# One attention block's first MLP matrix, batch 0: seven products of blocks in place of eight

## The chip, the cores and the metric

The kernel runs on one core of a Trainium2 chip. The time is the device time of one execution in microseconds (us), median of several runs. The engines are TensorE (PE in the profile; its weight loads are PEld), VectorE (DVE), ScalarE (ACT), GpSimd (POOL) and SyncE (SP), which here only issues DMAs. Each engine executes its own instructions in the order in which they are written; semaphores order them against the other engines.

## What is computed

One block of cross-attention with an MLP, in float32, for a batch of 4, 512 rows, width 512, 16 heads of 32:

```
x   = layer_norm(hidden, ln1_w, ln1_b)
q   = x @ q_w + q_b;   k = enc @ k_w + k_b;   v = enc @ v_w + v_b
p   = softmax(q k^T / sqrt(32)) per head, masked;   out = (p v) @ cproj_w + cproj_b
hid = out + hidden
y   = layer_norm(hid, ln2_w, ln2_b)
y   = gelu(y @ fc_w + fc_b)            # fc: 512 -> 2048
out = hid + y @ proj_w + proj_b        # proj: 2048 -> 512
```

## The kernel before

**Units.** Attention is cut into 16 weeks `w` (a batch `b` and four of its heads), each with 4 units (128 query rows, `qt`); unit number u = 4w + qt. In a unit, `scores` makes four 128x512 score products on TensorE into one PSUM tile `sc` (line 259), VectorE takes mask and minimum from it (263), ScalarE exponentiates (267), and `turn` transposes in blocks of 32 on VectorE (282, 290, 291); in odd units ScalarE also spreads the reciprocal sums (`rr`, 289). Two units' results are exchanged across partitions by sixteen DMAs of SyncE (`copies`, 325) into the tile `pT`, of which there is one, and `attend` (342) multiplies them with `v` two units or more later; VectorE then normalises (`oT`, 347), which frees `pT` for the next exchange. In the weeks from 5 to 12 there is an attend ahead of every even unit.

**Filler.** Between the units TensorE does the rest: `prep_k`, `prep_q`, `prep_v` of later weeks (215, 225, 237), the output projection `cproj` (383), the turning of normalised rows (156), and the MLP of batch 0 and half of fc and proj of batch 1: `fc` (449) and `proj` (459). Lists `first[w]` and `later[w]` name these items with a planned cost (`CHAIN` = 3.4, `TURN` = 0.5). Where the list is a tuple, its parts go to the four units as written; otherwise `run` (725) hands out items while half of the next cost fits into what is due. `some(n)` takes the next n items of the MLP's own list.

**fc before.** A chain `fc(b, f)` makes 128 of the 2048 columns: four 128x512 products in one PSUM tile of the ring `acc` (four banks), then one gelu on ScalarE straight from PSUM into `gT` (450). Weights come through a ring of eight slots `mlp_w`; `load_mlp` (441) is called after each chain and loads into the slots that are through. Exp and gelu need different tables on ScalarE; each change shows as an ACT_TABLE_LOAD.

**Norm of batch 0.** In unit 20, statistics on VectorE (125), then GpSimd takes the reciprocal root (`rs`, 133), VectorE normalises (147), and in unit 21 TensorE turns the four parts (`ln2_turn`); ScalarE and VectorE write `yT` from them (161, 159). On GpSimd's queue stand also `v_bias` (249), `add_row` (354), stores of `h` (386, 465) and loads of the mask (191).

**Last stage.** After attention, `last_mlps` does the rest of batches 1 to 3 by blocks: a product of 2x2 blocks with seven block products in place of eight (Strassen's scheme in Winograd's form). `fc_pair` (541) takes two chains at once: sums of weight blocks (`sum_wa`, lines 481 and 484, on VectorE), sums of blocks of `yT` (`y_sums`, 641), seven products of 128x256 (553), a copy of the first to `p1` (564), four adds on VectorE (531), four gelus of 128x256 (557). `project` (584) does the second matrix alike (593).

The lines that say how seven products make four blocks, in the code before (`product(o, a, y)` is two matmuls):

```python
product(q1[:, 0], a11, y11)
product(q62[:, 1], a12, y21)
product(q62[:, 0], s2, t2)
add(nc.vector, uc, q62, p1[:, None, :].broadcast_to([P, 2, HL]))
product(q75[:, 0], s3, t3)
product(q75[:, 1], s1, t1)
add(nc.vector, u34, q75, uc[:, :1].broadcast_to([P, 2, HL]))
add(nc.vector, uc[:, 0], q75[:, 1], u34[:, 0])
product(q43[:, 1], s4, y22)
product(q43[:, 0], a22, t4)
add(nc.vector, h, q43, u34)
```

Of the kernel before, what the change touches and what calls it, by code (L numbers as in the profile page):

```python
# [52 lines left out]
def xattn_block(ctx: ExitStack, tc: tile.TileContext, x, encT, mask, q_w, k_w, v_w, c_w, fc_w, p_w, vecs, rows, out):  # L53
# [3 lines left out]
    def pools(stack, **bufs):  # L57
        return [stack.enter_context(tc.tile_pool(name=n, bufs=k)) for n, k in bufs.items()]
# [28 lines left out]
    pb = pbt.rearrange("p (c i n) -> p c i n", c=NF // 2, i=2)  # L87
    pt = ptt.rearrange("p (s c n) -> p s c n", s=3, c=NF // 2)

    def k_q(w, i):  # L90
        n = w % 4 * 2 + i
        return pbt[:, n * D : (n + 1) * D]
# [18 lines left out]
        return ptt[:, n * D : (n + 1) * D].rearrange("p (d f) -> p d f", d=ND)  # L111

    S = {}
    count = [0, 0, 0]
    Q = [nc.sync]

    def acc_tile(name):
        return ps_acc.tile([P, D], F32, tag="acc", name=name)
# [315 lines left out]
    def load_mlp():  # L434

        while count[0] < len(weights) and (count[0] < MW or weights[count[0] - MW][3] < count[1]):
            name, b, f, _ = weights[count[0]]
            w = mlp_w(count[0])
            if name == "fc":
                w = w.rearrange("p (d f) -> p d f", d=ND)  # L440
            Q[0].dma_start(out=w, in_=fc_w[:, f, :, :] if name == "fc" else p_w[ts(f, P), :])
            S[name + "w", b, f] = w
            count[0] += 1

    def fc(b, f):
        q, k = divmod(f, FQ)
        acc = acc_tile(f"accf_{b}_{f}")
        for d in range(ND):
            nc.tensor.matmul(acc, S["fcw", b, f][:, d, :], S["yT", b][:, d, :], start=(d == 0), stop=(d == ND - 1))  # L449
# [20 lines left out]

    NP = NF // 2
    HL = L // 2

    def sub(o, x0, x1):  # L480
        nc.vector.tensor_tensor(o, x0, x1, ALU.subtract)  # L481

    def a_sums(a11, a12, a21, a22, s1, s2, s3, s4):
        nc.vector.tensor_tensor(s1, a21, a22, ALU.add)
        sub(s3, a11, a21)
        sub(s2, s1, a11)
        sub(s4, a12, s2)

    def b_sums(b11, b12, b21, b22, t1, t2, t3, t4):
        sub(t1, b12, b11)  # L490
        sub(t2, b22, t1)
        sub(t3, b22, b12)
        sub(t4, b21, t2)


    wa = [gt[:, i * 2048 : i * 2048 + 1024].rearrange("p (i d f) -> p i d f", i=2, d=ND) for i in range(2)]
# [14 lines left out]
        b_sums(b11, b12, b21, b22, pt[:, 0, c], pt[:, 1, c], b12, pt[:, 2, c])  # L511

    def last_mlps():
        last, ring = pools(ctx, last=1, ring=2)
        ps_last = ctx.enter_context(tc.tile_pool(name="ps_last", bufs=4, space=PSUM))
        ys = last.tile([P, 4, 2, HL], F32, tag="ys", name="ys")
# [7 lines left out]
        def half_tile(name):  # L524
            return ps_last.tile([P, 2, HL], F32, tag="half", name=name)

        def acc_half(name):
            return acc_tile(name).rearrange("p (i l) -> p i l", i=2)

        def add(engine, o, x0, x1):  # L530
            engine.tensor_tensor(o, x0, x1, ALU.add)  # L531

        def y_blocks(b):
            return [S["yT", b][:, 2 * k : 2 * k + 2, j * HL : (j + 1) * HL] for k in range(2) for j in range(2)]
# [6 lines left out]
        def fc_pair(b, c, first, sums):  # L541
            a11, a12, a21, a22 = (wa[c % 2][:, i, 2 * k : 2 * k + 2] for i in range(2) for k in range(2))
            y11, y12, y21, y22 = y_blocks(b)
            s1, s2, s3, s4 = (ws[c % 2][:, i] for i in range(4))
            t1, t2, t3, t4 = (ys[:, i] for i in range(4))
            q1, q62 = (acc_half(f"{n}_{b}_{c}") for n in ("q1", "q62"))
            q75, q43 = (half_tile(f"{n}_{b}_{c}") for n in ("q75", "q43"))
            p1 = ring.tile([P, HL], F32, tag="p1", name=f"p1_{b}_{c}")
            uc, u34, h = (ring.tile([P, 2, HL], F32, tag=n, name=f"{n}_{b}_{c}") for n in ("uc", "u34", "h"))

            def product(o, a, y):
                for k in range(2):
                    nc.tensor.matmul(o, a[:, k], y[:, k], start=(k == 0), stop=(k == 1))  # L553

            def gelu(i, j, src):
                f = 2 * c + i
                nc.scalar.activation(  # L557
                    ga[:, c, i, j * HL : (j + 1) * HL], src, AF.Gelu_apprx_tanh,
                    bias=vec[:, FCB + f : FCB + f + 1], scale=1.0,
                )  # L560

            sums()
            product(q1[:, 0], a11, y11)
            nc.scalar.copy(p1, q1[:, 0])  # L564
            product(q62[:, 1], a12, y21)

            if first:
                product(q43[:, 1], s4, y22)
            product(q62[:, 0], s2, t2)
            add(nc.vector, uc, q62, p1[:, None, :].broadcast_to([P, 2, HL]))  # L570
            gelu(0, 0, uc[:, 1])
            product(q75[:, 0], s3, t3)
            product(q75[:, 1], s1, t1)
            add(nc.vector, u34, q75, uc[:, :1].broadcast_to([P, 2, HL]))
            add(nc.vector, uc[:, 0], q75[:, 1], u34[:, 0])
            gelu(1, 1, uc[:, 0])
            if not first:
                product(q43[:, 1], s4, y22)
            product(q43[:, 0], a22, t4)
            add(nc.vector, h, q43, u34)  # L580
            gelu(1, 0, h[:, 0])
            gelu(0, 1, h[:, 1])
# [58 lines left out]
        def y_sums(b):  # L641
            b_sums(*y_blocks(b), *(ys[:, i] for i in range(4)))

        y_sums(SPLIT)

        half = FIRST * FQ // 2
        for b, pairs, new in (
            (SPLIT, range(half, NP), ()), (SPLIT + 1, range(NP), range(half)), (SPLIT + 2, range(NP), ())
        ):
            for c in pairs:  # L650
                if c in new:
                    for i in range(2):
                        nc.sync.dma_start(out=pb[:, c, i, :], in_=p_w[ts(2 * c + i, P), :])
                fc_pair(b, c, c == pairs[0], lambda: sum_wa(c + 1) if c + 1 < NP else None)
# [132 lines left out]
    mlp += FC(SPLIT, 0) + FC(SPLIT, 1) + PJ(SPLIT, 0) + PJ(SPLIT, 1)  # L787

    def some(n):
        taken, mlp[:n] = mlp[:n], []  # L790
        return taken

    def hid_(b, *ts_):
# [14 lines left out]
    def stat(b, *ts_):  # L808
        return do(lambda: [stat2(b, t) for t in ts_])

    def norm(b, *ts_):
# [133 lines left out]
```

## Time and profile before

| | |
|---|---|
| median of 3 runs | 810.84 us (810.18 to 811.25) |
| the profiled execution's own time | 810.09 us |
| its span, first to last instruction | 808.3 us |
| granted TensorE clock, mean | 0.996 |
| TensorE busy | 791.9 us |
| VectorE, ScalarE, GpSimd busy | 553.6, 360.8, 98.0 us |
| fc of batch 0 on TensorE | from 179.7 us to 387.5 us, between the units |
| last stage | from 558.5 us to the end |

A line of the timeline gives start and length in us, engine, line of the code, operation, the tiles written and read, the shape, how many records were merged, and in brackets how long the engine had stood idle before and what released it. `PE` lines are matmul records; one call of `nc.tensor.matmul` here makes two. SPq lines are DMA issues of SyncE.

### The profile page before, as it was taken

How to read it: one execution, taken by the hardware profiler on the slowest of the kernel's cores; microseconds unless marked ns; L12 is line 12 of the kernel's file. 1: busy time of each engine (PE TensorE's matmuls, PEld its weight loads, DVE VectorE, ACT ScalarE, POOL GpSimd, SP SyncE). 2: the span in 40 equal slices, each digit the busy share in tenths (PEclk: the TensorE clock that was granted, in tenths of full speed). 3: DMA queues.
4: the chain of work that ended last, by engine and by line, in shares of the span. 5: the costliest groups of instructions: out<-in, count | busy, mean ns of one | idle time of the engine just before them, and what ended most of it. 6: DMA issues, size and time to landing. Idle time of an engine off the chain costs nothing.

```text
span 808.3 us, 11790 instructions
## 1 busy us (share of the span) xinstructions
PE 791.9 (98%) x4082; PEld 481.2 (60%) x4082; DVE 553.6 (68%) x1145; ACT 360.8 (45%) x785; POOL 98.0 (12%) x112
## 2 busy tenths in 40 slices
PE   9999999979999999999999999999999999999998
PEld 6545455544454544535554333446888888888887
DVE  3788998876678665877778997636738993368511
ACT  2666755638673646556643469600312330023200
POOL 1110030030000030001131000120050021200011
PEclk9999999989999999999999999999999999999999
DMA  9889989837797877778768799883335330023001
GB/s 329 287 222 244 241 219 265 225 96 185 185 245 176 223 201 191 176 197 201 177 140 218 196 259 226 216 252 117 108 100 181 107 117 14 27 79 92 1 14 39
DMA packets 60955, 137.13 MB, mean 170 GB/s; under 512 B 12464, under 2 KB 15664, under 8 KB 60768
## 3 DMA queue, kind: packets, MB, share of 16 engines
q1 hardware_dynamic: 59472, 132.43, 61.2%
q0 software_dynamic: 896, 2.82, 1.1%
q10 hardware_dynamic: 528, 1.14, 0.7%
q8 instruction: 32, 0.52, 0.3%
q14 instruction: 27, 0.22, 0.1%
HBM read 58.22 MB, written 6.82 MB: 80 GB/s over the span
## 4 chain that ended last, share of the span: by engine, by line
PE 80%; DVE 7%; SPq 7%; DMA 3%; issue 1%; POOL 0%; ACT 0%; DVEq 0%; POOLq 0%
PE q L553 15%; PE accf L449 9%; PE accp L459 8%; PE accc L383 7%; SPq L325 7%; PE av L342 6%; PE sc L259 6%; PE acck L215 4%; PE accq L225 4%; PE accv L237 4%; DVE ptt L263 3%; PE q5p L593 2%; PE q3p L593 2%; PE q7p L593 2%; PE q6p L593 2%; PE q1p L593 2%
## 5 line engine op out<-in xcount | busy, mean ns | idle before, releaser
L267 ACT ACTIVATE ptt<-ptt,mn 128x512 f32<-128x512 f32 x256 | 182.2, 713 | 142.8 <-DVE mn L263 142.6
L263 DVE CUSTOM_DVE_ANT_0 ptt<-sc,mb 128x512 f32<-128x512 f32 x256 | 161.1, 685 | 45.6 <-PE sc L259 45.5
L282 DVE STREAM_TRANSPOSE tb<-ptt 128x1024 f32<-128x1024 f32 x96 | 119.1, 1242 | 10.4 <-ACT ptt L267 8.0
L449 PE MATMUL accf<-yT,pbt 128*128 128x512 f32 x192 | 87.3, 601 | 0.0
L459 PE MATMUL accp<-pbt,gt 128*128 128x512 f32 x192 | 86.5, 600 | 0.0
L259 PE MATMUL sc<-pbt 32*128 32x512 f32 x512 | 73.1, 640 | 4.8 <-DVE mn L263 2.6
L553 PE MATMUL q<-ys,gt 128*128 128x256 f32 x320 | 75.1, 379 | 0.0
L553 PEld LDWEIGHTS q<-ys,gt 128*128 128x128 f32 x320 | 60.8, 190 | 8.3
L449 PEld LDWEIGHTS accf<-yT,pbt 128*128 128x128 f32 x192 | 35.0, 190 | 50.2 <-issue 45.4
L459 PEld LDWEIGHTS accp<-pbt,gt 128*128 128x128 f32 x192 | 35.2, 190 | 48.8 <-issue 45.8
L237 PEld LDWEIGHTS accv<-ptt,xe 128*128 128x128 f32 x512 | 58.9, 192 | 8.2 <-issue 5.4
L237 PE MATMUL accv<-ptt,xe 128*128 128x128 f32 x512 | 60.5, 276 | 0.0
L215 PE MATMUL acck<-xe,ptt 128*128 128x512 f32 x128 | 59.0, 603 | 0.0
L553 PE MATMUL q<-yT,gt 128*128 128x256 f32 x240 | 58.1, 379 | 0.5 <-DVE gt L481 0.5
L225 PE MATMUL accq<-xe,ptt 128*128 128x512 f32 x128 | 58.4, 599 | 0.0
L383 PE MATMUL accc<-wc,oT 128*128 128x512 f32 x128 | 56.6, 596 | 0.0
L249 POOL TENSOR_TENSOR v<-v,row 128x512 f32<-128x512 f32 x16 | 20.4, 1274 | 278.5 <-ACT v L242 278.4
L557 ACT ACTIVATE ga<-uc,vec 128x256 f32<-128x256 f32 x40 | 20.4, 511 | 75.5 <-DVE uc L531 75.5
L553 PEld LDWEIGHTS q<-yT,gt 128*128 128x128 f32 x240 | 45.5, 190 | 7.4 <-DVE gt L481 0.9
L342 PE MATMUL av<-pT,v 128*32 128x256 f32 x768 | 48.1, 392 | 1.6 <-DMA pT<-tb 1.5
L267 ACT ACTIVATION_READ_ACCUMULATOR ptt<-ptt,mn 128x1 f32 x256 | 48.3, 189 | 0.0
L564 ACT COPY p<-q 128x256 f32<-128x256 f32 x20 | 7.1, 354 | 92.0 <-PE q L553 92.0
(121 smaller groups left out, 957.9 us busy)
## 6 DMA issues: line engine op xcount, KB each, us to landing
pT<-tb SPq DMA_DIRECT2D x384, 136.0 KB, 2.4
pbt<-p_w_dram SPq DMA_DIRECT2D x40, 256.0 KB, 3.1
gt<-fc_w_dram SPq DMA_DIRECT2D x40, 256.0 KB, 2.7
gt<-tb SPq DMA_DIRECT2D x64, 136.0 KB, 3.4
xe<-tb SPq DMA_DIRECT2D x56, 136.0 KB, 3.3
pbt<-fc_w_dram SPq DMA_DIRECT2D x24, 256.0 KB, 4.3
ptt<-k_w_dram SPq DMA_DIRECT2D x16, 256.0 KB, 3.9
xe<-encT_dram SPq DMA_DIRECT2D x16, 256.0 KB, 4.8
```

Source lines behind the costliest of these rows:

```text
L215: nc.tensor.matmul(acc, S["wk", w][:, d, :], eT[:, d, :], start=(d == 0), stop=(d == ND - 1))
L225: nc.tensor.matmul(acc, S["wq", w][:, d, :], xT[:, d, :], start=(d == 0), stop=(d == ND - 1))
L237: nc.tensor.matmul(acc[:, ts(t, P)], eT[:, d, ts(t, P)], S["wv", w][:, d, :], start=(d == 0), stop=(d == ND - 1),)
L259: nc.tensor.matmul(sc[:, h, :], qT[r, ts(qt, P)], kT[r, :], start=True, stop=True)
L263: nc.vector.tensor_tensor_reduce(out=s, in0=sc[:, h, :], in1=S["mb", w // NG], scale=1.0, scalar=FMAX, op0=ALU.add, op1=ALU.min, accum_out=mn,
L267: nc.scalar.activation(s, s, AF.Exp, bias=mn, scale=-1.0, accum_out=sums[:, qt, h : h + 1])
L282: nc.vector.transpose(*two_heads[k])
L342: nc.tensor.matmul(av[ts(h, HD), : 2 * P].rearrange(shape, **kw), v[:, t, ts(h, HD)], p[t][h], start=(t == 0), stop=(t == NT - 1),)
L383: nc.tensor.matmul(acc, S["oT", b][:, g, ts(t, P)], wc[:, g, :], start=(g == 0), stop=(g == NG - 1))
L449: nc.tensor.matmul(acc, S["fcw", b, f][:, d, :], S["yT", b][:, d, :], start=(d == 0), stop=(d == ND - 1))
L459: nc.tensor.matmul(acc, gT[q % 2][:, k, ts(t, P)], S["pw", b, q * FQ + k], start=(k == 0), stop=(k == FQ - 1))
L553: nc.tensor.matmul(o, a[:, k], y[:, k], start=(k == 0), stop=(k == 1))
```

## The change

The functions for sums and for seven products move out of `last_mlps` and get one body, `fc_seven`, for both places. fc of batch 0 uses it between the units, in pairs of chains (`fc_by_pair`). The sums of weight blocks are made by GpSimd (`fc_sums`), two pairs ahead; one of the four overwrites a block of the raw weights in their slot. The sums of blocks of `yT` of batch 0 are made half by VectorE and half by GpSimd, at the end of unit 21; one overwrites a block of `yT`. `fc_seven` adds into `g` itself and does the two gelus of 128x512 at its end, in place; in the last stage this replaces the four of 128x256, and the fourth product of a batch's first pair is no longer drawn forward. A pair is planned with 5.95; one list moves an item of fc from week 7 to week 8. The scratch space for GpSimd's own DMAs is set to 4096.

```diff
+    ys = const.tile([P, 3, 2, L // 2], F32, tag="ys", name="ys")
+    wsum = const.tile([P, 2, 3, 2, P], F32, tag="wsum", name="wsum")
...
+    def a_sums(a11, a12, a21, a22, s1, s2, s3, s4, engine=None):
+        add(engine or nc.vector, s1, a21, a22)
+        sub(s3, a11, a21, engine)
+        sub(s2, s1, a11, engine)
+        sub(s4, a12, s2, engine)
...
+    def y_sums(b):
+        y11, y12, y21, y22 = y_blocks(b)
+        e = nc.vector if b else nc.gpsimd
+        sub(ys[:, 0], y12, y11)
+        sub(ys[:, 1], y22, ys[:, 0])
+        sub(y12, y22, y12, e)
+        sub(ys[:, 2], y21, ys[:, 1], e)
...
+    def fc_seven(b, c, g, a, s, half):
+
+        y11, t3, y21, y22 = y_blocks(b)
+        t1, t2, t4 = (ys[:, i] for i in range(3))
+        s1, s2, s3, s4 = s
+        q1, q26 = (acc_half(f"{n}_{b}_{c}") for n in ("q1", "q26"))
+        q57, q34 = (half(f"{n}_{b}_{c}") for n in ("q57", "q34"))
+        p1 = small.tile([P, HL], F32, tag="p1", bufs=1, name=f"p1_{b}_{c}")
+        g = g.rearrange("p i (j l) -> p (i j) l", j=2)
...
+        product(q1[:, 0], a[0][:, 0:2], y11)
+        nc.scalar.copy(p1, q1[:, 0])
+        product(q26[:, 0], a[0][:, 2:4], y21)
+        product(q26[:, 1], s2, t2)
+        add(nc.vector, g[:, 0:4:3], q26, p1[:, None, :].broadcast_to([P, 2, HL]))
+        product(q57[:, 1], s3, t3)
+        product(q57[:, 0], s1, t1)
+        u2 = g[:, 3:4]
+        add(nc.vector, g[:, 1:3], q57, u2.broadcast_to([P, 2, HL]))
+        add(nc.vector, g[:, 3], q57[:, 0], g[:, 2])
+        product(q34[:, 0], s4, y22)
+        product(q34[:, 1], a[1][:, 2:4], t4)
+        add(nc.vector, g[:, 1:3], q34, g[:, 1:3])
+        for i in range(2):
+            f = 2 * c + i
+            h = g[:, 2 * i : 2 * i + 2]
+            nc.scalar.activation(h, h, AF.Gelu_apprx_tanh, bias=vec[:, FCB + f : FCB + f + 1], scale=1.0)
...
+    def fc_sums():
+
+        while count[3] < len(fc_pairs) and count[3] < count[4] + 2:
+            b, c = fc_pairs[count[3]]
+            if ("fcw", b, 2 * c + 1) not in S:
+                return
+            x, y = raw_pair(b, c)
+            s = wsum[:, count[3] % 2]
+            a_sums(x[:, :2], x[:, 2:], y[:, :2], y[:, 2:], s[:, 0], s[:, 1], y[:, :2], s[:, 2], nc.gpsimd)
+            S["ws", b, c] = s[:, 0], s[:, 1], y[:, :2], s[:, 2]
+            count[3] += 1
...
+    def fc_by_pair(b, c):
+        q, k = divmod(2 * c, FQ)
+        fc_seven(b, c, gT[q % 2][:, k : k + 2, :], raw_pair(b, c), S["ws", b, c], acc_half)
+        count[1] += 2
+        count[4] += 1
+        load_mlp()
+        fc_sums()
...
     def FC(b, q):
+        if b < SPLIT:
+            return [(2 * CHAIN * 7 / 8, lambda c=c: fc_by_pair(b, c)) for c in range(q * FQ // 2, (q + 1) * FQ // 2)]
         return [(CHAIN, lambda f=f: fc(b, f)) for f in range(q * FQ, (q + 1) * FQ)]
...
     first[5] = (
-        [k] + stat(0, 0, 1, 2, 3) + rs(0) + x3 + norm(0, 0, 1, 2, 3) + [v], [q] + t2, some(2) + pb_(0), some(2)
+        [k] + stat(0, 0, 1, 2, 3) + rs(0) + do(fc_sums) + x3 + norm(0, 0, 1, 2, 3) + [v], [q] + t2 + do(lambda: y_sums(0)), some(2) + pb_(0), some(2)
     )
...
-    first[7] = [k, q] + x2[:1] + some(2) + x2[1:2] + some(3) + [v]
+    first[7] = [k, q] + x2[:1] + some(2) + x2[1:2] + some(2) + [v]
...
-    first[8] = h_(1, 0, 1) + x2[2:] + [k, q] + x3[:2] + some(1) + x3[2:3] + [v] + x3[3:] + h_(1, 2, 3) + x4
+    first[8] = h_(1, 0, 1) + x2[2:] + [k, q] + x3[:2] + some(2) + x3[2:3] + [v] + x3[3:] + h_(1, 2, 3) + x4
...
-    nc = bacc.Bacc("TRN2", target_bir_lowering=False, num_devices=1)
+    nc = bacc.Bacc("TRN2", target_bir_lowering=False, num_devices=1, dynamic_dma_scratch_size=4096)
```

More of the change, by code (lines that the diff above doesn't have):

```diff
@@ L113, in xattn_block @@
     S = {}
-    count = [0, 0, 0]
+    count = [0, 0, 0, 0, 0]
     Q = [nc.sync]
@@ L443, in load_mlp, with sub, add, b_sums @@
             count[0] += 1
+    NP = NF // 2
+    HL = L // 2
+    def sub(o, x0, x1, engine=None):
+        (engine or nc.vector).tensor_tensor(o, x0, x1, ALU.subtract)
+    def add(engine, o, x0, x1):
+        engine.tensor_tensor(o, x0, x1, ALU.add)
+    def a_sums(a11, a12, a21, a22, s1, s2, s3, s4, engine=None):
[3 more added lines that the diff above has]
+        sub(s4, a12, s2, engine)
+    def b_sums(b11, b12, b21, b22, t1, t2, t3, t4):
+        sub(t1, b12, b11)
+        sub(t2, b22, t1)
+        sub(t3, b22, b12)
+        sub(t4, b21, t2)
@@ new lines, in y_blocks, with acc_half, product @@
+    def y_blocks(b):
+        return [S["yT", b][:, 2 * k : 2 * k + 2, j * HL : (j + 1) * HL] for k in range(2) for j in range(2)]
+    def y_sums(b):
[5 more added lines that the diff above has]
+        sub(ys[:, 2], y21, ys[:, 1], e)
+    def acc_half(name):
+        return acc_tile(name).rearrange("p (i l) -> p i l", i=2)
+    def fc_seven(b, c, g, a, s, half):
[6 more added lines that the diff above has]
+        g = g.rearrange("p i (j l) -> p (i j) l", j=2)
+        def product(o, x, y):
+            for k in range(2):
+                nc.tensor.matmul(o, x[:, k], y[:, k], start=(k == 0), stop=(k == 1))
+        product(q1[:, 0], a[0][:, 0:2], y11)
[15 more added lines that the diff above has]
+            nc.scalar.activation(h, h, AF.Gelu_apprx_tanh, bias=vec[:, FCB + f : FCB + f + 1], scale=1.0)
@@ new lines, in xattn_block, with raw_pair @@
+    fc_pairs = [(b, c) for b in range(SPLIT) for c in range(NP)]
+    def raw_pair(b, c):
+        return [S["fcw", b, 2 * c + i] for i in range(2)]
+    def fc_sums():
[8 more added lines that the diff above has]
+            count[3] += 1
@@ L467, in proj @@
         load_mlp()
[L477 to L493, printed above, removed]
+        fc_sums()
     wa = [gt[:, i * 2048 : i * 2048 + 1024].rearrange("p (i d f) -> p i d f", i=2, d=ND) for i in range(2)]
@@ L513, in last_mlps @@
     def last_mlps():
-        last, ring = pools(ctx, last=1, ring=2)
+        last, = pools(ctx, last=1)
         ps_last = ctx.enter_context(tc.tile_pool(name="ps_last", bufs=4, space=PSUM))
-        ys = last.tile([P, 4, 2, HL], F32, tag="ys", name="ys")
         ga = last.tile([P, NP, 2, L], F32, tag="ga", name="ga")
@@ L525, in half_tile @@
             return ps_last.tile([P, 2, HL], F32, tag="half", name=name)
[L527 to L534, printed above, removed]
         def g_sums(c):
@@ L539, in g_sums, with fc_pair @@
             a_sums(a11, a12, a21, a22, gs[:, 0, c], gs[:, 1, c], a21, gs[:, 2, c])
[L541 to L560, printed above, removed]
-            sums()
[L563 to L582, printed above, removed]
+        def fc_pair(b, c, sums):
+            sums()
+            fc_seven(b, c, ga[:, c], [wa[c % 2][:, i] for i in range(2)],
+                     [ws[c % 2][:, i] for i in range(4)], half_tile)
         def project(b, pairs, sums, turns, middle):
@@ L639, in project @@
                 nc.sync.dma_start(out=out[b, ts(2 + t, P), :HL], in_=hid(1, 0, t))
-        def y_sums(b):
-            b_sums(*y_blocks(b), *(ys[:, i] for i in range(4)))
         y_sums(SPLIT)
@@ L653, in last_mlps @@
                         nc.sync.dma_start(out=pb[:, c, i, :], in_=p_w[ts(2 * c + i, P), :])
-                fc_pair(b, c, c == pairs[0], lambda: sum_wa(c + 1) if c + 1 < NP else None)
+                fc_pair(b, c, lambda: sum_wa(c + 1) if c + 1 < NP else None)
                 if c + 2 < NP:
@@ L789, in some @@
     def some(n):
-        taken, mlp[:n] = mlp[:n], []
+        taken = []
+        while n > 0:
+            n -= 1 if mlp[0][0] == CHAIN else 2
+            taken.append(mlp.pop(0))
+        assert n == 0
         return taken
```

## The prediction

> **What bounds the kernel now.** I read the page's busy shares first, then TensorE's instructions in order of time, then the waits, then the DMA issues of SyncE's queue. TensorE is busy for 791.9 of 808.3 us:
>
> ```profile
> PE 791.9 (98%) x4082; PEld 481.2 (60%) x4082; DVE 553.6 (68%) x1145; ACT 360.8 (45%) x785; POOL 98.0 (12%) x112
> ```
>
> Only 16 us are left in which TensorE does nothing, so a change gains by giving it fewer or shorter products, and loses by making it wait. In the stretch that the change touches, TensorE's timeline (start, length, engine, line, tiles, count, idle before) has nearly no holes:
>
> ```profile
> 204.87 1.14 PE L259 MATMUL sc<-pbt 32*128 32x512 f32 x8
> 205.94 7.13 PE L449 MATMUL accf<-yT,pbt 128*128 128x512 f32 x16
> 213.00 1.93 PE L342 MATMUL av<-pT,v 128*32 128x256 f32 x32
> 214.87 1.14 PE L259 MATMUL sc<-pbt 32*128 32x512 f32 x8
> 215.94 3.70 PE L449 MATMUL accf<-yT,pbt 128*128 128x512 f32 x8
> ...
> 227.84 1.93 PE L342 MATMUL av<-pT,v 128*32 128x256 f32 x32
> ...
> 369.30 1.93 PE L342 MATMUL av<-pT,v 128*32 128x256 f32 x32 [0.98 <-DMA pT<-tb]
> ```
>
> There is a second bound just behind it. Each attend (`av`) frees the one `pT` tile, and SyncE then issues the sixteen DMAs that fill it for the next attend:
>
> ```profile
> 215.45 10.37 SPq L325 DMA_DIRECT2D pT<-tb  x16
> ...
> 355.87 11.39 SPq L325 DMA_DIRECT2D pT<-tb  x16
> ```
>
> A DMA here takes 0.63 us to issue and lands a median 2.4 us later. From the start of one attend to the earliest start of the next: 2.45 (attend 1.86, normalising multiply, until the first issue) + 9.4 (fifteen issues) + 2.4 (landing) + 0.24 (until TensorE starts) = 14.5 us. Where the issue took 11.39 instead of 10.03, the next attend really waited (the 0.98 above). The attends at 213.00 and 227.84 are 14.84 apart: hardly any slack.
>
> **The saving on TensorE.** Two chains of fc (16 records; a call of 128x512 is two of them) take 213.00 - 205.94 = 7.06 us, of which 0.2 belongs to the switch from the score products; 6.86 is pure. A pair by seven products is what the last stage does already:
>
> ```profile
> 570.58 1.89 PE L553 MATMUL q<-yT,gt 128*128 128x256 f32 x8
> 572.31 2.75 PE L553 MATMUL q<-ys,gt 128*128 128x256 f32 x12
> 574.90 1.03 PE L553 MATMUL q<-yT,gt 128*128 128x256 f32 x4
> 575.76 1.03 PE L553 MATMUL q<-ys,gt 128*128 128x256 f32 x4
> 576.63 1.89 PE L553 MATMUL q<-yT,gt 128*128 128x256 f32 x8
> ```
>
> 576.63 - 570.58 = 6.05 us for 28 records of 256 columns, 0.216 each: half of 0.429 for 512 columns. So a pair saves 0.81 us, eight pairs **6.5 us**. Weight loads don't spoil this between the attention units either: `accv` puts 32 records with 31 loads into 3.57 us there, 0.11 each.
>
> [...]
>
> **What is added, by engine.** VectorE gets four adds a pair: three of 128x512 from PSUM (0.69 each) and one of 128x256 (0.42), 2.5 us. In the unit at 204.87 it ends its transposes at 211.42 and is idle for 3.58 us, until the next `oT` at 215.00. There the adds fit. The cover ends where pairs follow each other, below. ScalarE gets a copy of 0.35 a pair and gelus as before, but these now come after VectorE's last add, some 0.9 us after the pair's end instead of overlapping it. GpSimd gets four sums a pair at 0.72 (row: 128x256 `hid<-u3p,hid`), 2.9 us, 23 us in all. They are issued two pairs ahead, 18 us or more before use, and the later weights come long before their pair (fc 8 and 9 are loaded near 212 and used near 270). I cost them at nothing. Should GpSimd take twice 0.72 it is still hidden. `y_sums`: two subtractions of 0.69 on VectorE after the last `yT` (about 175.8) and two of 1.27 on GpSimd, ready near 180; the third product wants the second sum at 181.5, the last product the fourth at 185. Free. GpSimd's smaller DMA scratch space: no row shows it; its 13 DMAs are off the path, at worst each waits for the landing of the one before (3.3 us) on GpSimd alone, and `v_bias` behind it has over 30 us to spare. I take 0, bounds 0 to 3.
>
> **New waits and what stands behind them.** VectorE's last add waits for the pair's last product; behind it are only the next attend's `oT` and the next unit's reductions, which TensorE releases later still. In unit 45 the four norms of batch 1 (0.5 each) stand between: `oT` comes 2.0 late, and attend 22 could start at 402.6 where TensorE reaches it at 403.1, so nothing is lost. GpSimd's sums wait for a weight's landing; behind them is `v_bias`. SyncE's next weight loads, formerly one after each chain, come as two after each pair and wait for its end; behind them is the exchange, which can't start before `oT`, some 2.4 us after the pair, and two issues take 1.0. Free.
>
> **Lock between GpSimd and VectorE.** The first eight sums are issued right after `rs`, beside the norms of batch 0, and those stand in the chain to a TensorE idle of 3.64 us:
>
> ```profile
> 164.13 4.86 DVE L147 TENSOR_SCALAR xn<-h,mv,rs 128x512 f32<-128x512 f32 x4 [1.40 <-POOL rs L133]
> ...
> 164.17 1.27 POOL L249 TENSOR_TENSOR v<-v,row 128x512 f32<-128x512 f32 x1
> ...
> 173.89 1.11 PE L156 MATMUL tp<-ident,xn 128*128 128x128 f32 x4 [3.64 <-ACT pbt L228]
> ```
>
> Alone a norm takes 0.53 (`h<-h`, `xn<-xn`); here four take 4.86, since each waits out a GpSimd operation. What follows (scores, exps, the last turn at 173.89) moves with their end. Now the operations beside them are 0.72 long instead of 1.27: taking turns, one waits 0.72 and then takes 0.4, four end after 4.4, a gain of 0.4. Bounds: no conflict, 4 x 0.53 = 2.1 (gain 2.7); locked out until all eight are through, 5.8 + 4 x 0.45 = 7.6 (loss 2.7). I take the turns, **-0.4**, as 165.8 to 169 shows them.
>
> [...]
>
> **Order of the units.** A pair now stands as one item of 5.95 in the planner instead of two of 3.4. Worked through its budgets, fc of pair 3 lies wholly in unit 26, `v` alone in 27; fc 8 leaves unit 31 and becomes part of pair 4 in unit 33; pair 5 lies with `k` in 37; one `proj` stands alone in 41 and the other goes with pair 6 into 42. Start to start, attends (numbered in order, 11 is the one at 213.00) then come:
> - 11 to 12: 14.84 - 0.81 = 14.0, below 14.5. With the issue of 10.37 that this stretch had, attend 12 waits **+0.8** (bounds 0.3 to 2.1).
> - 13 to 14 (18.3 becomes 14.6), 17 to 18 (14.8, as before) and 18 to 19 (18.1 becomes 14.7): just above 14.5, **+0.3** together; with a disturbed issue (11.39) each could cost 1.0 to 1.2.
> - 19 to 20: 14.84 + the wait became 15.88; with pair 6 inside it is 17.5 and the wait is gone, **-1.0**.
>
> **Back-to-back pairs.** Pair 0 and pair 1 lie in units 22 and 23 with only the scores between. Gelus of pair 0 end near 188.5, the exp table load (1.28) at 189.8, where exps could have begun at 187.9; four exps, a copy of `rr`, and the copy of `p1` ends at 193.7. It frees the bank that attend 10 writes, which TensorE reaches at 193.4: **+0.3**. (PSUM's `acc` ring has four banks and a pair takes all four.)
>
> **Last stage.** The fourth product is no longer drawn forward in a batch's first pair. Batch 1: TensorE reaches the third product 1.73 us after 558.50, its input `ys` is done near 560.8: +0.6. Batch 2: it waited at 611.17 for `s4`; now the wait is for `s2`, done 0.35 to 0.7 earlier: -0.4. Gelu of the last pair comes as one 128x512 after the last add, ready 1.55 us after the pair; batch 1 has four pairs, and `q1p` wants it after 3 x 0.43 = 1.3: +0.25; batches 2 and 3 want it after 3.0. Together **+0.4**. A gelu of 128x512 (0.69) for two of 0.51 frees ScalarE, which isn't on the path.
>
> **Sum.** -6.5 - 0.4 + 0.8 + 0.3 - 1.0 + 0.3 + 0.4 = -6.1. The profiled execution took 810.09 (span 808.3 + 1.8 around it), so 804.0; the median shown is 0.75 above that execution: **804.8**.
>
> **Rivals.** 0.2% is 1.6 us, about what a measurement can tell from no change: faster means below 809.2, slower above 812.5.
> 1. The forecast, 804.8, by itself 803 to 806.5: 0.58.
> 2. The exchange of `pT` takes the saving. For: four periods within 0.5 us of 14.5, and weight loads in twos just ahead of the exchange, as ahead of the 11.39. Against: most issues took 10.03. If two of the four are disturbed: 804.8 + 2.4 = 807.2; all four, 809.5: 0.18, a quarter of it above 809.2.
> 3. The eight sums lock VectorE out: 804.8 + 3.1 = 807.9. Against: turns were taken. 0.06.
> 4. Conflict mostly gone and waits beyond 1.0 recovered: 802.2. 0.08.
> 5. Slower: `p1`, gelus and table loads stand in ScalarE's one queue, and each pair holds all four banks until VectorE and ScalarE come round. `p1`'s copy ends 5.75 us after the scores begin if exps start at once, and the pair ends at 7.4; so it decides from a delay of 1.65 us. At pair 1 that is just reached. If it hit 1.0 us and more behind each of the eight pairs, 804.8 + 8 x 1.0 = 812.8. Against: elsewhere `k`, `q`, an attend or `v` lies between. 0.06.
> 6. It doesn't do what it says: products of 256 columns lose their 0.81 between units, for instance by a wait for GpSimd's sums in each pair, 810.8 or so: 0.04.
>
> Faster: 0.58 + 0.135 + 0.06 + 0.08 = 0.855, less a little for the ends of 3: 0.85. Same 0.09, slower 0.06. The range takes in rivals 3 and 4 and the milder half of 2: 802.0 to 808.4.
>
> **What would show it.** Right: 28 records of fc in about 6.05 + 0.2 us in units 22 to 45; a wait below 1 us at attends 10 and 12; none at 20; norms of batch 0 in 4 to 5 us. Wrong: waits of the product's weight loads for GpSimd, a 7 us block of norms, attends 14, 18 and 19 waiting 1 us each, or TensorE waiting for ScalarE's copy behind every pair.

## The result, and the profile after

| | before | after |
|---|---|---|
| median | 810.51 us (809.38 to 811.25) | 802.36 us (801.93 to 802.90, 4 runs) |
| ratio | | 0.9901, 95% interval 0.9884 to 0.9918 |
| profiled execution, its span | 810.09, 808.3 | 801.93, 800.2 |
| granted TensorE clock, mean | 0.996 | 0.998 |
| TensorE busy | 791.9 us | 785.3 us |

The kernel became faster by 8.1 us, 1%; the forecast was 6.1 (804.8, range 802.0 to 808.4). The span and the median shrank alike, 8.1 us each, so the two profiled executions can be set against each other.

The page's busy shares of the changed kernel:

```profile
PE 785.3 (98%) x4178; PEld 499.4 (62%) x4178; DVE 573.8 (72%) x1179; ACT 339.5 (42%) x745; POOL 123.9 (15%) x146
```

TensorE lost 6.6 us of work, although it executes 96 records more (each pair has 28 in place of 16). VectorE took 20 us more and GpSimd 26, ScalarE 21 less (30 table loads for 38 at 1.28 each, and in the last stage 40 wide gelus for 80 narrow ones, 26.7 us for 38.6). The load that rose is on the engines that have slack.

TensorE's timeline of the changed kernel shows the pair that stands where the prediction showed two chains (205.94 to 213.00 before), and the attends 9, 10, 11 and 12:

```profile
172.68 0.66 PE L159 MATMUL tp<-ident,xn 128*128 128x128 f32 x4 [3.05 <-ACT pbt L231]
173.35 3.61 PE L345 MATMUL av<-pT,v 128*32 128x256 f32 x32
...
192.28 1.93 PE L345 MATMUL av<-pT,v 128*32 128x256 f32 x32 [0.69 <-ACT p L498]
...
203.35 1.99 PE L495 MATMUL q<-yT,pbt 128*128 128x256 f32 x8
205.18 1.03 PE L495 MATMUL q<-ys,wsum 128*128 128x256 f32 x4
206.05 1.03 PE L495 MATMUL q<-yT,pbt 128*128 128x256 f32 x4
206.91 1.03 PE L495 MATMUL q<-ys,wsum 128*128 128x256 f32 x4
207.77 1.03 PE L495 MATMUL q<-yT,wsum 128*128 128x256 f32 x4
208.64 1.03 PE L495 MATMUL q<-ys,pbt 128*128 128x256 f32 x4
209.59 1.93 PE L345 MATMUL av<-pT,v 128*32 128x256 f32 x32
...
223.98 1.93 PE L345 MATMUL av<-pT,v 128*32 128x256 f32 x32 [0.30 <-issue]
```

209.59 - 203.35 = 6.24 us against 7.06, so 0.82 less. No product waits for GpSimd's sums (`wsum`) or for `ys`. Two of the attends wait: attend 10 for ScalarE's copy of `p1` (it holds the bank), and attend 12 for 0.30 us, for which the profile names no releaser (`issue`). By the times it is the exchange of `pT`: SyncE's last issue for it starts near 221.5, and a landing takes a median 2.4. SyncE's issues for attends 12 and 20 of the changed kernel:

```profile
212.05 10.03 SPq L328 DMA_DIRECT2D pT<-tb  x16
...
347.34 10.05 SPq L328 DMA_DIRECT2D pT<-tb  x16
```

Both were longer before (10.37, 11.39). In the changed execution none of the eleven issues for the attends from 12 to 22 took longer than 10.31, where the execution of before had three from 10.37 to 11.45.

**Where the time came from.** The starts of the same instructions in both timelines give the shift at each place; items that only moved between two attends are gone at the next place listed.

| TensorE starts | before | after | shift | what lies between |
|---|---|---|---|---|
| attend 8 | 151.52 | 151.67 | +0.15 | |
| attend 9 | 174.93 | 173.35 | -1.58 | norms of batch 0, their turns |
| attend 10 | 194.87 | 192.28 | -2.59 | pairs 0 and 1; its wait |
| attend 11 | 213.00 | 209.59 | -3.41 | pair 2 |
| attend 12 | 227.84 | 223.98 | -3.86 | pair 3; its wait |
| attend 16 | 302.31 | 297.71 | -4.60 | pair 4 |
| attend 17 | 320.44 | 315.02 | -5.42 | pair 5 |
| attend 20 | 369.30 | 362.01 | -7.29 | pair 6; the old wait of 0.98 |
| attend 21 | 387.44 | 379.32 | -8.12 | pair 7 |
| attend 23 | 419.37 | 410.81 | -8.56 | the old wait of 0.48 |
| first product of the last stage | 558.50 | 549.61 | -8.89 | `proj`, `cproj` |
| its second pair | 564.54 | 556.38 | -8.16 | first pair of batch 1 |
| `q2p` | 586.12 | 578.47 | -7.65 | last pair, gelu |
| second pair of batch 2 | 615.59 | 607.47 | -8.12 | first pair of batch 2 |

The pair terms are what was forecast. The first row with a surprise is attend 9, and there VectorE's and GpSimd's timelines of the changed kernel are to be read side by side. VectorE:

```profile
164.26 3.54 DVE L150 TENSOR_SCALAR xn<-h,mv,rs 128x512 f32<-128x512 f32 x4 [1.40 <-POOL rs L136]
```

GpSimd:

```profile
164.20 0.72 POOL L455 TENSOR_TENSOR wsum<-pbt 128x256 f32<-128x256 f32 x1
164.99 0.79 POOL L452 TENSOR_TENSOR pbt<-pbt 128x256 f32<-128x256 f32 x1
165.74 0.90 POOL L452 TENSOR_TENSOR wsum<-wsum,pbt 128x256 f32<-128x256 f32 x1
166.72 0.79 POOL L452 TENSOR_TENSOR wsum<-pbt,wsum 128x256 f32<-128x256 f32 x1
```

The four norms take 3.54 us, 1.32 less than before. GpSimd's `add_row` and TensorE's attend 9 before:

```profile
165.80 5.56 POOL L354 TENSOR_TENSOR h<-h,row 128x512 f32<-128x512 f32 x4 [0.36 <-DVE xn L147]
...
174.93 3.64 PE L342 MATMUL av<-pT,v 128*32 128x256 f32 x32
```

`add_row` no longer stands beside the norms: in GpSimd's queue it now comes behind the sums, `v_bias` and `y_sums`. The prediction did see shorter neighbours, and made too little of them.

The last stage of the changed kernel on TensorE:

```profile
549.61 1.89 PE L495 MATMUL q<-yT,gt 128*128 128x256 f32 x8
551.95 1.13 PE L495 MATMUL q<-ys,gt 128*128 128x256 f32 x4 [0.45 <-DVE ys L452]
...
574.50 1.46 PE L622 MATMUL q1p<-pbt,ga 128*128 128x256 f32 x6
576.21 2.43 PE L622 MATMUL q1p<-pbt,ga 128*128 128x256 f32 x10 [0.24 <-ACT ga L513]
```

Both foreseen waits are there: the third product waits for `ys`, and `q1p` for the last gelu.

### The profile page after: what moved, and what is told of

It reads as the page before. It is cut to its first block, busy times and chain, and to the rows that moved or that the text cites. A ratio compares the mean times of both kernels' runs of the same rounds, so it can differ in the third digit from the quotient of the medians.

```text
span 800.2 us, 12085 instructions
## 1 busy us (share of the span) xinstructions
PE 785.3 (98%) x4178; PEld 499.4 (62%) x4178; DVE 573.8 (72%) x1179; ACT 339.5 (42%) x745; POOL 123.9 (15%) x146
## 4 chain that ended last, share of the span: by engine, by line
PE 87%; DVE 6%; SPq 3%; ACT 1%; issue 1%; DMA 1%; POOL 0%; DVEq 0%; POOLq 0%; ACTq 0%
PE q L495 20%; PE accp L554 8%; PE sc L262 7%; PE accc L386 7%; PE av L345 7%; PE accv L240 6%; PE acck L218 6%; PE accq L228 5%; PE accf L536 3%; DVE ptt L266 3%; SPq L328 2%; PE q4p L622 2%; PE q3p L622 2%; PE q5p L622 2%; PE q6p L622 2%; PE q7p L622 2%
## 5 line engine op out<-in xcount | busy, mean ns | idle before, releaser
L495 PE MATMUL q<-yT,gt 128*128 128x256 f32 x320 | 78.9, 379 | 0.0
L513 ACT ACTIVATE ga<-ga,vec 128x512 f32<-128x512 f32 x40 | 26.7, 714 | 93.2 <-DVE ga L455 93.2
L495 PEld LDWEIGHTS q<-yT,gt 128*128 128x128 f32 x320 | 60.8, 190 | 8.7 <-issue 0.5
L495 PE MATMUL q<-ys,gt 128*128 128x256 f32 x240 | 61.8, 380 | 0.5 <-DVE ys L452 0.5
L495 PEld LDWEIGHTS q<-ys,gt 128*128 128x128 f32 x240 | 45.4, 190 | 7.4 <-DVE ys L452 0.9
L498 ACT COPY p<-q 128x256 f32<-128x256 f32 x28 | 9.9, 355 | 92.5 <-PE q L495 92.5
L228 PEld LDWEIGHTS accq<-xe,ptt 128*128 128x128 f32 x128 | 23.6, 190 | 32.4 <-issue 30.4
L262 PEld LDWEIGHTS sc<-pbt 32*128 32x128 f32 x512 | 20.0, 182 | 37.9 <-issue 21.4
```

Of the source, the lines that this page charges most:

```text
L228: nc.tensor.matmul(acc, S["wq", w][:, d, :], xT[:, d, :], start=(d == 0), stop=(d == ND - 1))
L262: nc.tensor.matmul(sc[:, h, :], qT[r, ts(qt, P)], kT[r, :], start=True, stop=True)
L495: nc.tensor.matmul(o, x[:, k], y[:, k], start=(k == 0), stop=(k == 1))
```

## The experiments

Each ratio is to the kernel before, run on the same chip beside the experiment. The median of before was 809.97 us beside e1 to e4, 810.32 beside e5 to e8, and 811.63 beside e3b. Theory: the gain is eight times 0.81 us of shorter products, and on top of it what the norms of batch 0 lose to GpSimd and to the clock. The rivals share the gain out otherwise: to the order of the units, to the scratch space, or to GpSimd being the engine that makes the sums.

### e1: eight products, but narrow

fc of batch 0 before, each wide product cut in two of 256 columns.

```diff
-        for d in range(ND):
-            nc.tensor.matmul(acc, S["fcw", b, f][:, d, :], S["yT", b][:, d, :], start=(d == 0), stop=(d == ND - 1))
+        for j in range(2 if b < SPLIT else 1):
+            o, y = (t[..., j * HL : (j + 1) * HL] if b < SPLIT else t for t in (acc, S["yT", b]))
+            for d in range(ND):
+                nc.tensor.matmul(o, S["fcw", b, f][:, d, :], y[:, d, :], start=(d == 0), stop=(d == ND - 1))
```

> The kernel before, with fc of batch 0 in products of 256 columns instead of 512 (eight calls a chain, twice the weight loads, no sums, same result). Theory A (the saving is that of the products: a call of 256 columns costs half of one of 512 between the units too): 16 chains x (8 x 0.432 - 4 x 0.857) = +0.4 us, so 810.9, within 0.2% of before. [...]

Measured: 810.62 us, ratio 1.0008 (0.9993 to 1.0023). TensorE's timeline of e1:

```profile
180.65 7.17 PE L451 MATMUL accf<-yT,pbt 128*128 128x256 f32 x32
187.75 1.14 PE L259 MATMUL sc<-pbt 32*128 32x512 f32 x8
188.83 7.17 PE L451 MATMUL accf<-yT,pbt 128*128 128x256 f32 x32
```

32 narrow records take 187.75 - 180.65 = 7.10 us between the units, where 16 wide ones took 7.06. Here a product of half the columns costs half, 0.503 of a wide one (7.10 / 2 / 7.06), so seven for eight saves an eighth. The sixth rival falls.

### e2: the kernel before, with `add_row` taken from beside the norms

```diff
-        [k] + stat(0, 0, 1, 2, 3) + rs(0) + x3 + norm(0, 0, 1, 2, 3) + [v], [q] + t2, some(2) + pb_(0), some(2)
+        [k] + stat(0, 0, 1, 2, 3) + rs(0) + x3 + norm(0, 0, 1, 2, 3) + [v], [q] + t2, some(2), some(2)
...
-    first[6] = [k, q] + some(4) + [v] + x1
+    first[6] = [k, q] + some(4) + [v] + pb_(0) + x1
```

> The kernel before with one thing moved: the four add_row of GpSimd on the residual of batch 0 stand behind the v_bias of week 9 instead of in unit 22, so that they no longer run beside the four norms of batch 0. Theory A (a part of the change's gain is not the seven products but that the norms meet shorter GpSimd operations): norms from 4.86 to about 3.2 us, the last turn 1.6 earlier, time 808.5 to 809. Rival B (that TensorE wait is set by something else): no change, 810.5.

Measured: 808.2 us, ratio 0.9974 (0.9955 to 0.9993). VectorE's timeline of e2:

```profile
165.97 2.98 DVE L147 TENSOR_SCALAR xn<-h,mv,rs 128x512 f32<-128x512 f32 x4 [1.40 <-POOL rs L133]
```

TensorE's:

```profile
173.84 0.66 PE L156 MATMUL tp<-ident,xn 128*128 128x128 f32 x4 [2.50 <-ACT pbt L228]
174.50 1.93 PE L342 MATMUL av<-pT,v 128*32 128x256 f32 x32
```

The norms fall from 4.86 to 2.98 us and TensorE's idle time from 3.64 to 2.50. The attend behind it takes 1.93 us, not 3.64: after the shorter idle time the clock wasn't halved (granted 1.00 from 166 to 176 us). So some 2 us of 810 (0.6 to 3.6 by the interval) were to be had without any product of blocks, by moving four additions in GpSimd's queue. The change has got most of the shorter norms, but in its profiled execution not the attend at full clock: behind its idle time of 3.05 us the attend still takes 3.61.

### e8: the order alone

The kernel before with the change's lists and pairs as items of 5.95, each pair still two chains of four wide products.

```diff
+        if b < SPLIT:
+            return [(2 * CHAIN * 7 / 8, lambda f=f: (fc(b, f), fc(b, f + 1))) for f in range(q * FQ, (q + 1) * FQ, 2)]
...
-    first[7] = [k, q] + x2[:1] + some(2) + x2[1:2] + some(3) + [v]
+    first[7] = [k, q] + x2[:1] + some(2) + x2[1:2] + some(2) + [v]
```

> The kernel before with the eight chains pairs of fc of batch 0 handed out as the change does it (two chains as one item of 5.95, lists of weeks 7 and 8 as changed), but made by eight wide products as before. Theory A (the order alone takes away the 1.0 us wait for pT before the attend at 369, and costs nothing else): -1.0 us, 809.5; the rest of the change's gain is products and norms. Rival B (a larger part of the gain is the order): 808 or less. Rival C (order costs): above 811.

Measured: 810.12 us, ratio 1.0003 (0.9993 to 1.0012). The attends 20 and 23 in TensorE's timeline of e8:

```profile
370.47 1.93 PE L342 MATMUL av<-pT,v 128*32 128x256 f32 x32
...
420.49 1.93 PE L342 MATMUL av<-pT,v 128*32 128x256 f32 x32 [0.44 <-DMA pT<-tb]
```

The wait at attend 20 is gone, as forecast, and still the median shows no gain. The reason is that the wait was never 1.0 us on the whole: the three other profiled kernels with the order of before have 0.41 (e1), 0.45 (e2) and 0.45 (e7) there. The 0.98 that the prediction read was the largest of four. From attend 10 to attend 21 e8 takes 191.73 us, the others 192.57 (before), 192.24, 192.04 and 192.04. What is left of the order's gain is 0.3 to 0.5 us, too little for these medians. The wait at attend 23 comes and goes likewise (0.48 before, 0.51 in e7, 0.44 in e8, none in e1 and e2). None of the six profiled executions with seven products has it; whether the change takes it away stays open.

### e7: the scratch space alone

```diff
-    nc = bacc.Bacc("TRN2", target_bir_lowering=False, num_devices=1)
+    nc = bacc.Bacc("TRN2", target_bir_lowering=False, num_devices=1, dynamic_dma_scratch_size=4096)
```

> The kernel before with only the scratch space of GpSimd's DMAs set to 4096. Theory A (off the path): 810.5, within 0.2%. Rival B (GpSimd's DMAs wait for each other and hold v_bias back): slower by 1 us or more, with waits on GpSimd near 428 to 440 us and 458 to 472 us.

Measured: 810.38 us, ratio 1.0000 (0.9989 to 1.0010). It costs nothing that shows. In the changed kernel, which has the same setting, GpSimd's waits between 421 and 464 us, where its own DMAs stand, are those of before (430 to 473) to within 0.02 us.

### e3 and e3b: the weight sums on VectorE

e3 is the changed kernel with its weight sums on VectorE at the same places; e3b also computes them only one pair ahead.

```diff
-            a_sums(x[:, :2], x[:, 2:], y[:, :2], y[:, 2:], s[:, 0], s[:, 1], y[:, :2], s[:, 2], nc.gpsimd)
+            a_sums(x[:, :2], x[:, 2:], y[:, :2], y[:, 2:], s[:, 0], s[:, 1], y[:, :2], s[:, 2])
```

e3b beside that:

```diff
-        while count[3] < len(fc_pairs) and count[3] < count[4] + 2:
+        while count[3] < len(fc_pairs) and count[3] < count[4] + 1:
```

> The changed kernel with the weight sums on VectorE instead of GpSimd, in the same places of the program. Theory A (GpSimd matters as a separate queue: the sums wait for weights to land, and VectorE would wait with its reductions behind them): at pair 3's sums VectorE waits some 6 us, at pair 2's 2 us, and TensorE loses most of it at the next scores; 13 us of extra VectorE work fit mostly into its idle time: 808 to 813. Rival B (VectorE has the room and waits nowhere): 802.4 to 803. Rival C (VectorE is full, all 13 us show): 815 and more.

> The changed kernel with the weight sums on VectorE, as in e3, but computed one pair ahead instead of two, so that the block of weights they read has been loaded when they are issued. Theory A (in e3 the loss came from sums that stood at the head of VectorE's queue and waited 10.9 us for weights, with the score and exchange work behind them): without that wait only the 32 sums of 0.42 us are left, 13.4 us on an engine that is idle a quarter of the time; 803 to 806 us, VectorE's wait for pbt<-fc_w_dram under 2 us, TensorE's waits for pT<-tb under 2 us. Rival B (VectorE has no room beside the attention units, and each of the eight groups of 1.7 us delays the exchange by itself): 809 to 816 us, with TensorE still waiting for pT<-tb or mn.

Measured: e3 814.93 us, ratio 1.0079 (1.0056 to 1.0103); e3b 803.08 us, ratio 0.9907 (0.9880 to 0.9934). The same 32 subtractions and additions on the same engine: some 12 us worse than the change in one place, not told from it in the other. VectorE's timeline of e3:

```profile
232.11 0.43 DVE L455 TENSOR_TENSOR wsum<-pbt 128x256 f32<-128x256 f32 x1 [6.17 <-DMA pbt<-fc_w_dram]
232.57 0.42 DVE L452 TENSOR_TENSOR pbt<-pbt 128x256 f32<-128x256 f32 x1
232.91 0.42 DVE L452 TENSOR_TENSOR wsum<-wsum,pbt 128x256 f32<-128x256 f32 x1
233.36 0.43 DVE L452 TENSOR_TENSOR wsum<-pbt,wsum 128x256 f32<-128x256 f32 x1
233.71 0.69 DVE L266 CUSTOM_DVE_ANT_0 ptt<-sc,mb 128x512 f32<-128x512 f32 x1
```

and TensorE's, beside it:

```profile
230.41 3.54 PE L345 MATMUL av<-pT,v 128*32 128x256 f32 x32 [3.37 <-DMA pT<-tb]
236.29 1.14 PE L262 MATMUL sc<-pbt 32*128 32x512 f32 x8 [2.34 <-DVE mn L266]
```

VectorE stands for 6.17 us before a sum whose weights haven't landed, and behind it in its queue stands the reduction of the scores, which was ready. This is TensorE's second wait, of 2.34. Its first, of 3.37, goes back to the pair before. There `oT`, which the exchange waits for, came only behind the four sums, 5.09 us after the start of attend 11 (212.96), where the change has 2.01 (211.60 - 209.59):

```profile
218.05 0.42 DVE L350 TENSOR_TENSOR oT<-av,pT 128x256 f32<-128x256 f32 x1
```

TensorE pays a third time in the attend itself: 3.54 us for 1.93, as in the change at attend 9 (3.61), where the granted clock was 0.50. Four such waits take 10.9 us of VectorE. Their entry among VectorE's waits of e3:

```profile
DVE wsum L455 <- DMA pbt<-fc_w_dram: 10.9, 4, 6.2
```

e3b has no wait of VectorE for weights among its larger ones, and at TensorE one wait of 1.4 us is left:

```profile
PE av L345 <- DMA pT<-tb: 1.4, 1, 1.4
```

So VectorE has room for the 13 us of sums but for some 1 us: from attend 10 to 12 e3b takes 33.09 us for the change's 31.70, and 0.4 of that comes back from its shorter norms (2.85). What GpSimd's separate queue buys is that a sum issued early may wait for its weights without standing in anyone's way: in the change GpSimd waits four times for them, 62.6 us in all and 19.0 the longest, and TensorE has no wait for a sum. The outcome of e3 lies 2 us above the range that the first theory had given (the slower attend alone is 1.6 of it) and next to the 815 of its rival C, that VectorE is full. By its time alone e3 couldn't decide; e3b does, and the rival (no room on VectorE) falls.

### e4: quiet norms

The changed kernel; the first eight sums move one week earlier (`first[4]`), and the `v_bias` of batch 2's first week moves behind `y_sums`, so that GpSimd is idle during the norms.

```diff
-        [k] + stat(0, 0, 1, 2, 3) + rs(0) + do(fc_sums) + x3 + norm(0, 0, 1, 2, 3) + [v], [q] + t2 + do(lambda: y_sums(0)), some(2) + pb_(0), some(2)
+        [k] + stat(0, 0, 1, 2, 3) + rs(0) + x3 + norm(0, 0, 1, 2, 3) + [v], [q] + t2 + do(lambda: (y_sums(0), v_bias(8))), some(2) + pb_(0), some(2)
...
-        if w:
+        if w not in (0, 8):
...
-    first[4] = x1 + [k, q, v] + x4
+    first[4] = do(fc_sums) + x1 + [k, q, v] + x4
```

> The changed kernel with the first eight weight sums in week 4 and the v_bias of week 8 behind y_sums on GpSimd's queue, so that GpSimd is idle beside the norms of batch 0. Theory A (the lock between the two engines sets how long the norms take, and they stand in the chain to TensorE's long wait): norms from 3.54 to 2.1 us, the wait of 3.05 us before the last turn shrinks to 1.7, and then the granted clock, which was 0.5 for 3.5 us after it, may stay at 1.0: -1.4, or -3.1 with the clock: 801.0 or 799.2. Rival B (norms are not in the chain or not slowed by GpSimd): 802.4.

Measured: 799.13 us, ratio 0.9871 (0.9845 to 0.9897). VectorE's timeline of e4:

```profile
165.09 1.92 DVE L150 TENSOR_SCALAR xn<-h,mv,rs 128x512 f32<-128x512 f32 x4 [1.41 <-POOL rs L136]
```

TensorE's:

```profile
171.89 0.66 PE L159 MATMUL tp<-ident,xn 128*128 128x128 f32 x4 [1.44 <-ACT pbt L231]
172.56 1.93 PE L345 MATMUL av<-pT,v 128*32 128x256 f32 x32
```

Undisturbed, the four norms take 1.92 us, so 0.48 each; the idle time halves and the attend runs at full clock (1.00 from 166 to 176 us). 3.54 - 1.92 = 1.62 and 3.61 - 1.93 = 1.68, together 3.3, the difference of the medians' distances from before (10.8 against 8.1) but for 0.6. Seven executions, by TensorE's idle time (us; an attend of 1.93 is one at full clock; e1, e7 and e8 are as before, e6 is as e4):

| kernel | four norms | TensorE idle | attend 9 |
|---|---|---|---|
| before | 4.86 | 3.64 | 3.64 |
| e3 | - | 3.63 | 3.52 |
| after | 3.54 | 3.05 | 3.61 |
| e3b | 2.85 | 2.64 | 3.13 |
| e5 (the changed kernel's code up to here) | 3.54 | 2.51 | 1.93 |
| e2 | 2.98 | 2.50 | 1.93 |
| e4 | 1.92 | 1.44 | 1.93 |

The length of the norms does not set the idle time alone: e3b has shorter norms than e2 and a longer idle time (2.64, 2.50), and in e3 the norms begin behind eight sums in VectorE's own queue. In e5 the last turn comes as late behind attend 8 as in the changed kernel (21.0 us); TensorE reached the wait 0.54 later, and the attend kept its full clock (1.00 from 170 to 176 us). So of e4's 3.3 us the 1.6 of the norms are its own, and the 1.7 of the clock can also fall to the changed kernel.

### e5 and e6: the last stage mended

e5 is the changed kernel with the two waits of the last stage taken out: in the first pair of batch 1 the product of `s4` comes ahead of the one that waits for `ys`, and in its last pair the first gelu is cut in two, one half issued as soon as its block is complete. e6 is e4 and e5 together.

```diff
+        if early:
+            product(q34[:, 0], s4, y22)
         product(q26[:, 1], s2, t2)
...
+        if split:
+            gelu(0, 0, 1)
         product(q57[:, 1], s3, t3)
...
-        product(q34[:, 0], s4, y22)
+        if not early:
+            product(q34[:, 0], s4, y22)
...
```

> The changed kernel with the last stage's two losses taken back for batch 1: its first pair makes the product of s4 early again, and its last pair does the gelu of the block that q1p needs first right after the first add. Theory A (they cost 0.7 at the first pair and 0.5 at q1p): both waits gone, -1.1 us, 801.2 by the median of the changed kernel, span 799.1. Rival B (the lost time there is hidden by something later): same as the changed kernel, 802.4.

> The changed kernel with both: quiet norms as in e4 and the last stage as in e5. Theory A (the two stand in different stretches of one chain and add): 799.1 - 1.1 = 798.0. Rival B (the second is hidden behind the first): 799.1.

Measured: e5 801.64 us, ratio 0.9895 (0.9880 to 0.9909); e6 799.65 us, ratio 0.9866 (0.9846 to 0.9886). By the medians neither is told from the kernel that it mends (802.36 and 799.13). The traces tell. TensorE's timeline of e5:

```profile
549.31 2.75 PE L501 MATMUL q<-yT,gt 128*128 128x256 f32 x12
551.90 1.03 PE L501 MATMUL q<-ys,gt 128*128 128x256 f32 x4
...
573.48 3.62 PE L635 MATMUL q1p<-pbt,ga 128*128 128x256 f32 x16
576.94 3.62 PE L635 MATMUL q2p<-pbt,ga 128*128 128x256 f32 x16
```

Neither has a wait in it: from the first product to `q2p` it takes 27.63 us, after the change 28.86, before 27.62. So the 1.2 us that the new body costs in batch 1 can be had back; from `q2p` to the end both take 221.7 us, so nothing later hides it. The other 0.3 us by which e5 is ahead lie before the last stage and are not its doing: with the same code up to there, its attend 9 ran at full clock (1.93 us) after an idle time of 2.51, and a wait of 1.18 at attend 14 took most of that back.

e4 and e6 are faster than the kernel before. Against the changed kernel their intervals (up to 0.9897 and 0.9886) overlap a little with its own (from 0.9884), and they did not run beside it; that they are ahead of it rests on the traces. Between the two the choice stays open.

## Why the prediction was right, and where it wasn't

The forecast named the likeliest case and its mechanism, and the time fell into the range, 2.4 us below the number. It lies below the 803 to 806.5 that the prediction gave to this case by itself, and on the 802.2 of its fourth rival, which the range had taken in. There is luck in it too: the other terms that it named miss by up to 0.4 each and cancel (+0.8 together, +0.7 measured), and two differences that nobody foresaw took a further 0.75. Step by step (predicted, measured in us):

| step | predicted | measured |
|---|---|---|
| eight pairs | -6.5 | -6.5 (0.81 to 0.82 each) |
| norms of batch 0 | -0.4 | -1.7 |
| attend 10, back-to-back pairs | +0.3 | +0.6 |
| attend 12, exchange | +0.8 | +0.4 |
| attends 14, 18, 19 | +0.3 | 0 |
| attend 20 | -1.0 | -1.1, of it some 0.5 by the order |
| last stage | +0.4 | +0.8 |
| attend 23; end of `proj` | none | -0.45; -0.3 |
| sum | -6.1 | -8.2 |

**Saving on TensorE**: right; e1 shows it by itself, with 0.503 of a wide product for a narrow one.

**What is added, by engine**: right. The adds of VectorE, the sums of GpSimd (0.72 to 0.91), `y_sums` and the scratch space cost nothing. The first sum of `y_sums` on GpSimd took 1.77 us, not 1.27; nothing waited for it. In unit 45 the norms of batch 1 cost nothing either (attend 22 has no wait).

**GpSimd beside the norms** (the prediction's lock): this is the mis-sized term, -0.4 for -1.7. "Taking turns, one waits 0.72 and then takes 0.4" makes 1.12 a norm; it took 0.885, and the sign that the prediction named, norms in 4 to 5 us, did not come. What is behind the step was not costed at all: "what follows moves with their end" treats the turns and the attend as fixed lengths. They ran at a granted clock of 0.50 (the stretches of before in the last section); with the earlier end, the turns (1.11 before, 0.66 after) came at full clock (1.00). The bound for no conflict (-2.7) was put too low too: in e4 the norms gain 2.94, and the attend's full clock gives a further 1.7.

What sets the length of the norms beside a busy GpSimd stays open: four norms took 2.98 beside one 1.27 operation of GpSimd (e2), 2.85 beside the same (e3b), 3.54 beside five of 0.72 to 0.91, 4.86 beside operations of 1.27 and more.

**Order of the units**: the waits at attends 12 and 20 were placed rightly, and the sizes were read too closely from one execution. Attend 12's period floor of 14.5 came out as 14.39 (223.98 - 209.59, with a wait of 0.30), with the issue at 10.03 instead of the 10.37 assumed. Attends 14 and 19 come 14.84 and 14.70 after the one before them, above the floor and without a wait (the 14.6 forecast for the first is a slip: 18.28 less a chain of 3.43 is 14.85). That none of the three waits is a matter of the execution: in e5, the same code up to there, attend 14 came 16.08 us after the one before it and waited 1.18 for the exchange, which is what the prediction gave for a disturbed issue. Of the 1.0 at attend 20 only 0.41 to 0.45 is there in three executions of four.

**Back-to-back pairs**: right in place and cause (a bank held by `p1`), twice the size: the copy ended at 192.23 and TensorE was there at 191.59. Both had been forecast later (193.7 and 193.4), TensorE more so, since the norms gave it more than thought.

**Last stage**: the right three waits, with +0.73 for +0.6, -0.47 for -0.4 and +0.51 for +0.25. In the last, 0.24 is the wait; the rest lies in the products around it.

Of the rivals, the fourth (conflict mostly gone, 802.2) came nearest in its number and half in its cause; the second shows in e5 at one attend; the third, fifth and sixth did not come. (The sixth's 810.8 should have read 811.3, 804.8 + 6.5.)

**What isn't explained**: the 0.3 us in a block of `proj` between attend 23 and the last stage (14.21 us before, 13.93 after). e7 and e8 take 13.93 there too, so it is not the change's; e1 has a wait of 0.28 for the weights of `proj` in that block. Nor is it explained why SyncE's issues are disturbed: to 11.39 and 11.45 us in the execution of before and to 11.50 in e7's, to 10.31 at most in the change's. From one execution to the next of the same first 150 us, attend 8 starts between 150.10 (e3b) and 153.82 us (e6), and on the kernel before and its variants between 151.52 and 153.37; a difference of a microsecond between two traces is not yet an effect.

## What to carry to other kernels

Where TensorE is the bound and products of half the width cost half (0.503 here), a seven-product scheme pays its eighth also in pieces between other work, provided that the sums stand in a queue in which they may wait. Before moving elementwise work to another engine, ask what stands behind it in its queue if its input is late; the same 32 operations cost some 12 us or about one. And look at the clock column behind every idle time of TensorE, here from 1.6 us on: the halved clock cost the run of products behind one 1.6 to 1.7 us (3.61 for 1.93, 5.47 for 3.84), as much as the shorter of these idle times.

## What the runs showed of the hardware

At attend 9 an idle time of TensorE of 2.64, 3.05 or 3.64 us (e3b, after, before) was followed by a granted clock of 0.50, and one of 3.63 (e1, e3, e7, e8) by an attend of 3.52 to 3.64 us; behind 2.51, 2.50 and 1.44 (e5, e2, e4) the clock stayed at 1.00 and the attend took 1.93. This is no threshold. In e3 a wait of 2.34 (at 236.29) was followed by eight products of `prep_k` in 5.40 us, which take 3.70 at 197.88. In e8 one of 1.63 (at 84.30) was followed by 32 products in 5.47 us, which take 3.84 behind the same wait of 1.63 in seven other executions (before, after, e1, e2, e4, e5, e6). TensorE's timeline of e8:

```profile
84.30 1.14 PE L259 MATMUL sc<-pbt 32*128 32x512 f32 x8 [1.63 <-DVE mn L263]
85.37 5.47 PE L237 MATMUL accv<-ptt,xe 128*128 128x128 f32 x32
```

The table of stretches of the changed kernel (start and end, length, then busy time of each engine, then the granted clock, then the DMA share and GB/s):

```profile
171.00:173.00 2.00, 0.32 (x3) 0.32 (x4) 1.99 (x5) 1.73 (x5) 0.91 (x1) 1.00 0.00 0
173.00:175.00 2.00, 1.99 (x20) 0.93 (x21) 2.00 (x4) 1.08 (x2) 0.00 (x0) 0.61 0.00 0
175.00:177.00 2.00, 2.00 (x24) 0.76 (x16) 0.74 (x2) 0.00 (x0) 1.81 (x2) 0.54 0.00 0
177.00:179.00 2.00, 2.00 (x13) 1.14 (x14) 1.32 (x4) 0.16 (x1) 1.19 (x1) 1.00 0.23 48
```

and of the kernel before:

```profile
172.00:174.00 2.00, 0.11 (x1) 0.11 (x2) 1.99 (x4) 1.73 (x5) 0.00 (x0) 0.50 0.00 0
174.00:176.00 2.00, 2.00 (x16) 1.20 (x20) 1.66 (x3) 1.28 (x2) 0.00 (x0) 0.50 0.00 0
...
178.00:180.00 2.00, 2.00 (x17) 0.70 (x10) 0.61 (x2) 0.00 (x0) 0.00 (x0) 0.81 0.00 0
```

In the changed kernel the clock still reads 1.00 while TensorE is idle, falls near 173.4, when it works again, and is back 3.4 us later. Before, it had fallen near 171.9, 2 us ahead of the work at 173.89, and stayed halved for 6.8 (both read from stretches of 0.1 us). So the length of a wait does not say by itself whether the clock falls. The price is paid by the instructions behind the wait, and no list of waits shows it.
